# First attention of a vision tower: the next block's key and value matmuls at other chunks of the block before

## The chip, the cores and the metric

The kernel runs on one core of one Trainium2 chip. The metric is the device time of one execution in microseconds, the median of several; a profiled execution beside them gives the instructions' times. A core has TensorE (PE, with its weight loads as PEld), VectorE (DVE), ScalarE (ACT), GpSimd (POOL), each with its own in-order program, and SyncE (SP), which here issues DMAs. TensorE writes its results into PSUM, from where ACT or DVE copy them.

## What is computed

The reference is a small vision tower: a tokenizer of two convolutions gives 128 images x 64 tokens x 256 features, and two pre-norm layers follow. The change touches the attention of the first layer, which has 8 groups of 32 features and compares queries with keys by a ReLU of their difference:

```python
Q = x @ Wq.T; K = x @ Wk.T; V = x @ Wv.T            # x: (B, L, 256), normalized
diff = Q.reshape(B, L, 1, G, Dg) - K.reshape(B, 1, L, G, Dg)
attn = jnp.einsum('bqkgd,d->bqkg', jax.nn.relu(diff), w_mlp) + b_mlp[0]
attn = jax.nn.softmax(jax.nn.relu(attn), axis=2)
out = jnp.einsum('bqkg,bkdg->bqdg', attn, V.reshape(B, L, Dg, G))
```

For one image that is 64 x 64 x 256 differences, so the elementwise work and its sum over the 32 features of a group fill the stage.

## The kernel before

All of it is fp32. The activations stay in SBUF as `h2`, with two images' tokens on the 128 partitions. `relu_attention` works in eight **blocks** of 16 images, and a block in eight **chunks** of 8 query positions, 64 chunks in all. In the trace the features lie on the partitions (two halves, `hf` 0 and 1) and a tile of differences has 8 queries x some images x 64 keys.

*What a chunk does.* The `relu(q - k)` tiles of a chunk are made by three engines. DVE makes five of them in one pass each (`relu`, L570). POOL makes three differences (`difference`, L586), which ACT makes positive in six halves (`positive`, L590). ACT makes two images' parts by itself, one query at a time, in four groups of four (`by_query`, L599). PE sums every part over its features into the score tile `sc` by matmuls with a 0/weight matrix (`add`, L612, whose matmul is recorded at L417). A call of `add` sums four images. The last two adds of a chunk are `add(4, 1)` and `add(8, 1, last=True)`.

*The softmax runs one chunk later.* While chunk n is made, DVE takes the row maximum of chunk n-1's scores (`maximum`, L616, then ACT at L617), subtracts it (L621), ACT takes the exponentials (L624), DVE sums and inverts (L627, L628), POOL multiplies (L631), PE transposes the weights (L642), and one chunk later still ACT copies them to `at` (L650). PE also computes the next chunk's queries (`queries`, recorded at L424 as `pc`), which ACT copies (L510).

*What a block needs.* Before its first chunk a block needs 8 normalized row tiles (statistics L83 and L84 on DVE, factors L93 to L96 on POOL, the normalization on ACT, L109, or POOL, L107), their transposes (`transpose` L441, copied by `transposed` L447), four **key calls** (`keys`, PE, 16 records of 128x512 named `pk`, copied by ACT in `keyed`, L468), and four **value calls** (`values`, PE, 32 records of 128x256 named `pv`, copied by ACT in `valued`, L486). All keys must be there when its first chunk begins, the values when its outcome is taken. The outcome (`outcome`, L523, copied at L539) is computed in the second chunk of the block that follows, and transposed back and added to `h2` (`back` L546, `added` L556 on DVE) in that block's third and fourth chunk.

*What sets the order.* The order is written out by hand: everything runs under a manual schedule, and each engine takes its instructions in the order in which the Python calls are made. Work that is not of the chunk itself is entered with `at(n, place, ...)` for chunk n (counted over all blocks; n is the first chunk of block b in `n - 4`) and a place in the chunk's list of calls. The places that matter here, in the list's order:

- "O": on ACT after `older.transposed` (L650), ahead of the second half of `by_query(14, 1)` and of L617
- "X": on PE after the first add
- "A": on ACT after the exponentials and the fourth of the six L590
- "Y": on PE after the third add, ahead of `add(12, 1)`
- "B": on ACT after L510, ahead of the eight L599 of `by_query(15, 1)`; the add of that image stands ahead of `add(4, 1)` on PE
- "Z": on PE after the transposes of the old weights (L642), ahead of `add(8, 1, last=True)`

So the last two calls of PE in a chunk, with "Z" between them, are:

```python
ch.add(4, 1)
if old:
    old.transpose()
do(n, "Z")
...
ch.add(8, 1, last=True)
```

PSUM tiles of all this side work share four buffers (tag "pq"), used in turn. The second block's work in the first block, and the start of the layer's second part (`beside`) in the last blocks, have entries of their own.

Of the kernel before, what the change touches and what calls it, by code (L numbers as in the profile page):

```python
# [22 lines left out]
B = 128  # L23
# [357 lines left out]
def relu_attention(c, sh, ready, wqkv, wmlp, bmlp, beside):  # L381
# [10 lines left out]
    with (  # L392
# [263 lines left out]
        def at(n, place, *steps):  # L656
            work.setdefault((n, place), []).extend(steps)

        def of(f, *a):
            return lambda: f(*a)  # L660
# [18 lines left out]
        for b, x in enumerate(blocks):  # L679
            n = 8 * b  # L680

            if b + 1 < len(blocks):
                at(n + 9, "X", of(x.outcome, 0))
                at(n + 9, "A", of(x.outcome_copied, 0, 0))
                at(n + 9, "B", of(x.outcome_copied, 0, 1))
                at(n + 9, "Y", of(x.outcome, 1))
                at(n + 9, "C", of(x.outcome_copied, 1, 0))
                at(n + 10, "O", of(x.outcome_copied, 1, 1))
                for i in range(4):
                    at(n + 10 + i // 2, "XY"[i % 2], of(x.back, i))  # L690
                    at(n + 10 + i // 2, ("V1", "V2")[i % 2], of(x.added, i))
            if b == 0:
                for i in range(4):
                    at(i // 2 * 2, "XY"[i % 2], of(x.values, i))
                    at(i // 2 * 2, "AB"[i % 2], of(x.valued, i))
                continue

            if b == 1:
                at(0, "V1", *(of(x.statistics, i) for i in range(NP)))
                at(0, "W", x.factors)  # L700
                at(0, "C", of(x.normal, 0), of(x.normal, 1))
                at(1, "X", of(x.transpose, 0))
                at(1, "A", of(x.normal, 2), of(x.transposed, 0))
                at(1, "B", of(x.normal, 3))
                at(1, "Z", of(x.transpose, 1))
                at(2, "O", of(x.transposed, 1))
                for i in range(2):
                    at(n - 6 + i, "A", of(x.normal, 4 + 2 * i))
                    at(n - 6 + i, "B", of(x.normal, 5 + 2 * i))
                    at(n - 6 + i, "Z", of(x.transpose, 2 + i))  # L710
                    at(n - 5 + i, "O", of(x.transposed, 2 + i))
                for fo in range(2):
                    at(n - 4 + fo, "X", of(x.keys, 0, fo))
                    at(n - 4 + fo, "A", of(x.keyed, 0, fo))
                    at(n - 4 + fo, "Z", of(x.keys, 1, fo))
                    at(n - 3 + fo, "O", of(x.keyed, 1, fo))
                for i, (k, place) in enumerate(((5, "Y"), (4, "Y"), (2, "X"), (1, "X"))):
                    at(n - k, place, of(x.values, i))
                    at(n - k, "BA"[place == "X"], of(x.valued, i))
                continue  # L720
            for i in range(NP):
                at(n - 21 + i if b > 2 else 1 + i // 4, "V2", of(x.statistics, i))
            at(n - 13, "W", x.factors)
            for i in range(4):
                at(n - 12 + i, "A", of(x.normal, i))
                at(n - 12 + i, "C", of(x.normal, 4 + i, nc.gpsimd))
            at(n - 9, "X", of(x.transpose, 0))
            at(n - 9, "A", of(x.transposed, 0))
            at(n - 9, "Z", of(x.transpose, 2))
            at(n - 8, "O", of(x.transposed, 2))  # L730
            at(n - 8, "X", of(x.transpose, 1))
            at(n - 8, "A", of(x.transposed, 1))
            at(n - 8, "Z", of(x.transpose, 3))
            at(n - 7, "O", of(x.transposed, 3))
            at(n - 7, "Z", of(x.keys, 0, 0))
            at(n - 6, "O", of(x.keyed, 0, 0))
            at(n - 6, "Y", of(x.values, 0))
            at(n - 6, "B", of(x.valued, 0))
            at(n - 6, "Z", of(x.keys, 1, 0))
            at(n - 5, "O", of(x.keyed, 1, 0))  # L740
            at(n - 5, "Y", of(x.values, 1))
            at(n - 5, "B", of(x.valued, 1))
            at(n - 5, "Z", of(x.keys, 0, 1))
            at(n - 4, "O", of(x.keyed, 0, 1))
            at(n - 4, "X", of(x.keys, 1, 1))
            at(n - 4, "A", of(x.keyed, 1, 1))
            for i in range(2):
                at(n - 3 + i, "X", of(x.values, 2 + i))
                at(n - 3 + i, "A", of(x.valued, 2 + i))

        for (n, place), steps in beside.items():
            at(n, place, *steps)
# [1630 lines left out]
@with_exitstack  # L2383
def vit_tower(ctx: ExitStack, tc: tile.TileContext, a, out):
    const = ctx.enter_context(tc.tile_pool(name="const", bufs=1))
    dram = ctx.enter_context(tc.tile_pool(name="dram", bufs=1, space=DRAM))
    c = Ctx(tc, const)

    hd = dram.tile([B, T, D], F32, name="hd")

    hx = dram.tile([B, T, D], F32, name="hx")
    gfd = dram.tile([B * T, 1], F32, name="gfd")
    with tc.tile_pool(name="stream", bufs=1) as sp:
        c.h2 = sp.tile([P, B // 2, D], F32, name="h2")
        front = Front(c, hd, *(a[k] for k in ("wqk1", "bqk1", "wv1", "bv1", "wg")))
        with ExitStack() as rings:
            np_ = rings.enter_context(tc.tile_pool(name="an", bufs=2))
            ready = tokenizer(c, a["x"], a["w1"], a["bn1"], a["w2"], a["bn2"], np_)
            sh = Shared(c, rings, ExitStack(), np_)
            beside, rest = expert_attention(  # L2400
                c, sh, front, hd, *(a[k] for k in ("normw", "wr", "br", "wqkvf", "wvf", "wproj", "bproj", "wout"))
            )
            rest(*relu_attention(c, sh, ready, a["wqkv0"], a["wmlp"], a["bmlp"], beside))
    c.tables(ctx.enter_context(tc.tile_pool(name="tables", bufs=1)))
    with tc.tile_pool(name="gate", bufs=1) as gp:
        k = Routing(c, gp, a["wg"], a["bg"])
        with front.ctx:
            linear_attention(c, front, hd, hx, out, k)
        experts(c, hx, gfd, out, a["we1"], a["we2"], a["be2"], lambda: route(c, k, gfd))
# [70 lines left out]
```

## Time and profile before

| | us |
|---|---|
| median of 3 runs | 2536.23 |
| the three runs | 2533.86, 2536.23, 2541.09 |
| profiled execution | 2531.03 |
| its span, first to last instruction | 2529.3 |
| first attention in it, from the first L570 to the last L616 | 173 to 1040 |

The profiled execution was 5.2 us below the median. Over its span PE is busy 95%, DVE 79%, POOL 66% and ACT 65%. Those shares are means over stages: the tokenizer up to 173 us, the first attention, then the rest of the two layers. In the first attention, 173.08 to 1040.50 us, PE is busy 827 of 867 us, DVE 822, ACT 799, POOL 791. A PE instruction is recorded from its start to a modelled end, and neighbours overlap (an L417 record lasts 0.60 us and four start in every 0.43), so a busy PE is not a PE at its peak. DMA moves 3 GB/s there.

### The profile page before, as it was taken

How to read it: one execution, taken by the hardware profiler on the slowest of the kernel's cores; microseconds unless marked ns; L12 is line 12 of the kernel's file. 1: busy time of each engine (PE TensorE's matmuls, PEld its weight loads, DVE VectorE, ACT ScalarE, POOL GpSimd, SP SyncE). 2: the span in 40 equal slices, each digit the busy share in tenths (PEclk: the TensorE clock that was granted, in tenths of full speed). 3: DMA queues.
4: the chain of work that ended last, by engine and by line, in shares of the span. 5: the costliest groups of instructions: out<-in, count | busy, mean ns of one | idle time of the engine just before them, and what ended most of it. 6: DMA issues, size and time to landing. Idle time of an engine off the chain costs nothing.

```text
span 2529.3 us, 88213 instructions
## 1 busy us (share of the span) xinstructions
PE 2397.4 (95%) x38809; PEld 1613.7 (64%) x38809; DVE 2007.6 (79%) x2935; ACT 1643.9 (65%) x3529; POOL 1679.4 (66%) x1299
## 2 busy tenths in 40 slices
PE   8989999999999999899999999999999869999997
PEld 4654444444444444577777777876666657888886
DVE  7879999999999999888889898887667794444443
ACT  3239999989999998777777777775544433232332
POOL 4339998989999998588788887853322404545453
PEclk9999999999999999999999999999999989999998
DMA  4000000000000000000000000001544434555553
GB/s 126 26 14 2 3 2 3 2 3 2 2 3 2 3 14 2 3 29 22 17 14 25 14 25 14 24 14 42 103 106 109 101 108 170 194 188 196 192 195 125
DMA packets 138071, 141.57 MB, mean 56 GB/s; under 512 B 108129, under 2 KB 121859, under 8 KB 129870
## 3 DMA queue, kind: packets, MB, share of 16 engines
q1 hardware_dynamic: 128684, 119.45, 15.8%
q0 software_dynamic: 7648, 14.77, 1.9%
q8 instruction: 307, 5.03, 0.8%
q10 hardware_dynamic: 1344, 1.61, 0.2%
q14 instruction: 88, 0.72, 0.1%
HBM read 103.97 MB, written 32.54 MB: 54 GB/s over the span
## 4 chain that ended last, share of the span: by engine, by line
PE 52%; DVE 20%; POOL 11%; ACT 8%; issue 6%; DMA 1%; SPq 0%; POOLq 0%; DVEq 0%; ACTq 0%
DVE m L570 9%; PE sc L417 7%; PE po L2322 6%; PE ph L2306 6%; POOL e L1209 5%; PE pc L231 4%; PE pq L1622 3%; PE pz L1232 3%; PE pqk L1099 2%; ACT m L590 2%; PE pt L1217 2%; PE pv L1636 2%; PE pv L1122 2%; PE pk L424 2%; ACT m L599 2%
## 5 line engine op out<-in xcount | busy, mean ns | idle before, releaser
L586 POOL TENSOR_TENSOR m<-q,k 128x2048 f32<-128x2048 f32 x192 | 691.4, 3627 | 19.0 <-ACT q L510 10.1
L570 DVE CUSTOM_DVE_ANT_1 m<-pc,k 128x2048 f32<-128x2048 f32 (+1 forms) x320 | 652.9, 2059 | 0.9 <-ACT q L510 0.5
L417 PE MATMUL sc<-m,wide 128*32 128x512 f32 x4096 | 589.3, 598 | 36.1 <-ACT m L590 12.9
L590 ACT ACTIVATE m<-m 128x1024 f32<-128x1024 f32 x384 | 383.9, 1049 | 0.3
L417 PEld LDWEIGHTS sc<-m,wide 128*32 128x32 f32 x4096 | 158.2, 109 | 310.0 <-issue 178.0
L599 ACT ACTIVATE m<-k,q 128x64 f32<-128x64 f32 x1024 | 265.0, 343 | 3.9 <-DVE k L466 3.9
L1209 POOL TENSOR_TENSOR e<-e,mx 128x1024 f32<-128x1024 f32 x127 | 241.6, 1903 | 9.9
L1222 ACT COPY pT<-pt 128x512 f32<-128x512 f32 x256 | 133.4, 597 | 109.6 <-PE pt L1217 109.6
L2306 PE MATMUL ph<-xt,w1s 128*128 128x256 f32 x896 | 200.5, 382 | 1.7 <-DVE xt L2297 1.1
L2322 PE MATMUL po<-w2s,hT 128*128 128x256 f32 x896 | 198.0, 379 | 0.0
L2306 PEld LDWEIGHTS ph<-xt,w1s 128*128 128x128 f32 x896 | 171.0, 191 | 26.8 <-DVE xt L2297 1.7
L2322 PEld LDWEIGHTS po<-w2s,hT 128*128 128x128 f32 x896 | 168.1, 190 | 21.7
L2340 POOL DMA_INDIRECT out<-y,rout x56 | 56.6, 1011 | 168.1 <-ACT hT L2310 129.1
L1191 DVE TENSOR_REDUCE mx<-sc 128x16 f32<-128x1024 f32 x128 | 150.3, 1215 | 21.3 <-PE sc L1181 21.2
L1201 DVE TENSOR_REDUCE mx<-e 128x16 f32<-128x1024 f32 x128 | 154.7, 1209 | 6.3 <-ACT e L1198 4.6
L2310 ACT ACTIVATE hT<-ph,w1s 128x256 f32<-128x256 f32 x224 | 93.0, 470 | 98.6 <-PE ph L2306 98.6
L1198 ACT ACTIVATE e<-e 128x1024 f32<-128x1024 f32 x128 | 133.6, 1060 | 34.9 <-DVE e L1195 29.3
L2327 ACT ACTIVATE y<-y,gf 128x256 f32<-128x256 f32 x56 | 28.0, 507 | 194.4 <-issue 107.2
L1195 DVE TENSOR_TENSOR e<-sc,mx 128x1024 f32<-128x1024 f32 x128 | 150.1, 1213 | 0.1
L1106 ACT COPY kr<-pqk 128x512 f32<-128x512 f32 x248 | 127.3, 601 | 23.9 <-PE pqk L1099 23.8
L1217 PE MATMUL pt<-ident,e 128*128 128x128 f32 x1024 | 130.4, 277 | 12.0 <-POOL e L1209 10.8
L1232 PEld LDWEIGHTS pz<-pT,vr 128*64 128x64 f32 x4096 | 124.7, 138 | 21.1 <-issue 10.9
(347 smaller groups left out, 4796.2 us busy)
## 6 DMA issues: line engine op xcount, KB each, us to landing
w1s<-in_we SPq DMA_DIRECT2D x30, 1028.0 KB, 5.1
w2s<-in_we SPq DMA_DIRECT2D x30, 1024.0 KB, 4.9
h<-hd SPq DMA_DIRECT2D x4, 2048.0 KB, 12.2
hx<-h SPq DMA_DIRECT2D x4, 2048.0 KB, 12.2
out<-h SPq DMA_DIRECT2D x4, 2048.0 KB, 20.4
xt<-in_x SPq DMA_DIRECT2D x15, 512.0 KB, 3.7
hd<-h SPq DMA_DIRECT2D x15, 512.0 KB, 3.7
x<-hd SPq DMA_DIRECT2D x12, 512.0 KB, 3.6
```

Source lines behind the costliest of these rows:

```text
L417: nc.tensor.matmul(dst[j : j + 32], wide[:, hf, s : s + 32], part, start=start, stop=stop)
L570: nc.vector._custom_dve(TENSOR_ADD_SAT, out=m, in0=bcast(self.pc[:, o : o + n * 8].rearrange("p (t i) -> p t i", i=n), 3, T), in1=bcast(se ...
L586: nc.gpsimd.tensor_tensor(m, bcast(self.q[:, hf, s : s + 4], 3, T), k, ALU.add)
L590: nc.scalar.activation(m, m, AF.Relu)
L599: nc.scalar.activation(self.parts[i, hf][:, q], self.blk.k[:, hf, i], AF.Relu, bias=self.q[:, hf, i - NB // 2, q : q + 1],)
L1191: nc.vector.tensor_reduce(mx, self.sc[x].rearrange("p h c s -> p (h c) s"), AX.X, ALU.max)
L1201: nc.vector.tensor_reduce(self.sm[x], self.e[x], AX.X, ALU.add)
L1209: eng.tensor_mul(e, e, bcast(sm, 2, T))
L1217: nc.tensor.transpose(pt[:, cq, :], e[:, i : i + 2, :].rearrange("p e s -> p (e s)"), c.ident)
L1232: nc.tensor.matmul(pz[par * 64 : par * 64 + 64, fc, t], self.v[:, par, r % 2, 2 * fc + j, r // 2 * 64 : r // 2 * 64 + 64], self.pT[r // 2] ...
L2306: nc.tensor.matmul(ph[:, j], self.w1[:, w0 : w0 + P], self.xt[:, fc], start=(fc == 0), stop=(fc == 1))
L2322: nc.tensor.matmul(po, self.hT[:, f, r * P : r * P + P], self.w2[:, f, :], start=(f == 0), stop=(f == 7))
```

## The change

In the general schedule (blocks 3 to 8), a block's four key calls and four value calls move within the block before. With that block's chunks counted from 1:

| call | before: chunk, place (copy) | after: chunk, place (copy) |
|---|---|---|
| keys (0,0) | 2, Z (3, O) | 5, X (5, A) |
| keys (1,0) | 3, Z (4, O) | 5, Z (6, O) |
| keys (0,1) | 4, Z (5, O) | 6, Z (7, O) |
| keys (1,1) | 5, X (5, A) | 7, Z (8, O) |
| values 0 | 3, Y (3, B) | 6, X (6, A) |
| values 1 | 4, Y (4, B) | 7, X (7, A) |
| values 2 | 6, X (6, A) | 8, Y (8, B) |
| values 3 | 7, X (7, A) | own 1, Y (1, B) |

For block 2 only the value calls move: from chunk 4 (Y, B), 5 (Y, B), 7 (X, A) and 8 (X, A) of the first block to 4 (Y, B), 7 (X, A), 8 (Y, B) and its own 1 (Y, B). Nothing is added or removed.

```diff
-                for i, (k, place) in enumerate(((5, "Y"), (4, "Y"), (2, "X"), (1, "X"))):
+                for i, (k, place) in enumerate(((5, "Y"), (2, "X"), (1, "Y"), (0, "Y"))):
                     at(n - k, place, of(x.values, i))
                     at(n - k, "BA"[place == "X"], of(x.valued, i))
                 continue
...
             at(n - 7, "O", of(x.transposed, 3))
-            at(n - 7, "Z", of(x.keys, 0, 0))
-            at(n - 6, "O", of(x.keyed, 0, 0))
-            at(n - 6, "Y", of(x.values, 0))
-            at(n - 6, "B", of(x.valued, 0))
-            at(n - 6, "Z", of(x.keys, 1, 0))
-            at(n - 5, "O", of(x.keyed, 1, 0))
-            at(n - 5, "Y", of(x.values, 1))
-            at(n - 5, "B", of(x.valued, 1))
-            at(n - 5, "Z", of(x.keys, 0, 1))
-            at(n - 4, "O", of(x.keyed, 0, 1))
-            at(n - 4, "X", of(x.keys, 1, 1))
-            at(n - 4, "A", of(x.keyed, 1, 1))
+            at(n - 4, "X", of(x.keys, 0, 0))
+            at(n - 4, "A", of(x.keyed, 0, 0))
+            at(n - 4, "Z", of(x.keys, 1, 0))
+            at(n - 3, "O", of(x.keyed, 1, 0))
+            at(n - 3, "X", of(x.values, 0))
+            at(n - 3, "A", of(x.valued, 0))
+            at(n - 3, "Z", of(x.keys, 0, 1))
+            at(n - 2, "O", of(x.keyed, 0, 1))
+            at(n - 2, "X", of(x.values, 1))
+            at(n - 2, "A", of(x.valued, 1))
+            at(n - 2, "Z", of(x.keys, 1, 1))
+            at(n - 1, "O", of(x.keyed, 1, 1))
             for i in range(2):
-                at(n - 3 + i, "X", of(x.values, 2 + i))
-                at(n - 3 + i, "A", of(x.valued, 2 + i))
+                at(n - 1 + i, "Y", of(x.values, 2 + i))
+                at(n - 1 + i, "B", of(x.valued, 2 + i))
```

## The prediction

> **What bounds it now.** I read the page's 40 slices first: the first attention is the stretch from 173 to 1040 us, slices 3 to 17, where PE and DVE (and ACT and POOL) stand at 8 or 9 tenths:
>
> ```profile
> PE   8989999999999999899999999999999869999997
> DVE  7879999999999999888889898887667794444443
> ```
>
> Busy shares separate nothing there, so I cut the stretch at an event that comes once a chunk: DVE's row maximum of the chunk before, line 616. A "step into chunk n" runs from that maximum in chunk n-1 to the one in chunk n. The windows view over the eight steps of block 5 (columns: window, length, then busy us and instructions of PE, PEld, DVE, ACT, POOL, then clock, DMA share, GB/s):
>
> ```profile
> 600.60:613.69 13.09, 11.99 (x185) 5.16 (x184) 12.54 (x13) 12.78 (x31) 12.90 (x6) 1.00 0.01 1
> 613.69:626.31 12.62, 11.92 (x188) 5.10 (x184) 12.55 (x12) 12.31 (x30) 11.85 (x5) 1.00 0.01 3
> 626.31:640.36 14.05, 13.88 (x454) 8.48 (x448) 12.55 (x12) 13.45 (x32) 13.02 (x5) 1.00 0.02 4
> 640.36:654.99 14.63, 14.58 (x239) 6.89 (x232) 13.71 (x13) 12.40 (x30) 11.84 (x4) 1.00 0.01 2
> 654.99:669.62 14.63, 14.58 (x239) 6.92 (x235) 13.71 (x13) 12.40 (x30) 11.66 (x8) 1.00 0.01 3
> 669.62:682.16 12.54, 12.27 (x200) 5.98 (x196) 12.47 (x11) 12.39 (x31) 12.54 (x6) 1.00 0.01 3
> 682.16:694.70 12.54, 12.27 (x213) 6.14 (x209) 12.47 (x13) 12.23 (x30) 12.54 (x6) 1.00 0.01 1
> 694.70:707.23 12.53, 12.24 (x213) 5.96 (x205) 12.46 (x12) 12.21 (x30) 12.53 (x6) 1.00 0.01 3
> ```
>
> The steps into chunks 6 to 8 (last three) are DVE's: 12.47 of 12.54 us busy. Those into 3, 4 and 5 are longer than DVE's work by 1.50, 0.92 and 0.92. Blocks 2 to 4 have the same lengths within 0.05, but for block 2's step into 1 (13.58) and gaps in PE's issue in the steps into 3 (14.33, 15.62, 16.09). The clock is 1.00 throughout. The chain of waits, followed over the end of the step into 5, says what makes a step long (start, us, what):
>
> ```profile
> 662.17 1.92 ACT m L599 x8
> 664.14 1.11 PE sc L417 x9
> 665.45 0.59 PE sc L417
> 666.05 0.73 PE pt L642 x49
> 666.94 1.72 PE pk L424 x13
> 668.66 0.87 PE sc L417 x8
> 669.62 0.69 DVE mx L616
> ```
>
> It is a loop. The maximum lets ACT's L617 go; ACT runs in order to its eight L599, whose result PE adds (L612, shown as 417); PE then transposes the old weights (642), does whatever stands at place "Z", here a key call of 1.72, and only then the last add of the scores that the next maximum reads. Without keys the loop is just closed: at 682.16 maximum; 682.88 L617; L599 ends at 690.69; maximum at 694.70. That is 0.72 + 7.81 + 4.01 = 12.54, as long as DVE's own work. So **a key call at "Z" has nothing to hide behind in a 12.5 us step**. The first block shows this directly: in it block 2's key calls already stand at "Z" of chunks 5 and 6. Its steps into chunks 7 and 8, by the windows view, and ACT's timeline at the end of the first:
>
> ```profile
> 249.78:263.83 14.05, 13.79 (x215) 6.80 (x211) 12.55 (x11) 12.77 (x31) 12.41 (x6) 1.00 0.01 2
> 263.83:276.38 12.55, 12.29 (x216) 6.25 (x212) 12.48 (x12) 12.40 (x31) 10.83 (x6) 1.00 0.01 2
> ```
>
> ```profile
> 255.12 0.57 ACT L468 ACTIVATE k<-pk 128x512 f32<-128x512 f32 x1
> 255.59 0.59 ACT L109 ACTIVATE xn<-h,nb,rs 128x256 f32<-128x256 f32 x1
> ...
> 262.90 0.60 ACT L468 ACTIVATE k<-pk 128x512 f32<-128x512 f32 x1 [1.13 <-PE pk L424]
> ```
>
> With keys 14.05, without 12.55, DVE equally busy in both: 1.50 per key call. A PSUM copy costs ACT 0.47 (255.12 to 255.59).
>
> **The change, step by step**, for a middle block. The same instructions run; DVE, POOL and SP keep their order, no DMA moves, and each of the four shared PSUM buffers is copied out before its turn comes again, so no new wait from there.
>
> - Into chunk 3: the key call at "Z" of chunk 2 goes. Next late is DVE, 12.55: from 14.05, **-1.50**. Bounds: 0 (the 256 records of the outcome matmuls in chunk 2 keep PE the bound, as 13.88 busy hints) and -1.50. I take -1.50: in block 6 PE reaches the transposes at 743.26, and L599 lets it go no earlier (741.35 and 1.8 of adds). The gaps in PE's issue I leave as they are.
> - Into 4 and 5: a key call at "Z" and a value call at "Y" go from each, with ACT's wait of 0.95 for the value matmuls in front of L599 (662.07). Next late is DVE, whose 13.71 holds the two additions of L556: 13.75, **-0.88** twice. Bounds 0 and -0.92.
> - Into 6, 7 and 8: each gets a key call at "Z" (of chunks 5, 6, 7), and ACT the key copy at "O", behind which stand half of the L599 and L617. **+1.52** each, to 14.06. Bounds: 0 (a gain is excluded, since DVE's 12.47 stays) and +1.72, the whole call. I take the row 14.05, which has the same ACT work: two copies at "A" and the key copy.
> - Into 6 besides: GpSimd. After the normalization factors of chunk 4 POOL is busy without a break from 661.24; its second L586 of chunk 5 ends at 672.15, that is 17.16 after chunk 4's maximum. ACT wants it at 672.45, 2.83 after chunk 5's maximum. With that step 13.75 long it comes 3.41 after it: ACT waits **+0.58**. Bounds 0 and 0.58; the nearest row is the first block, where the third L590 of chunk 5 starts 1.13 after the second and not 0.95: 0.18 for POOL. I take 0.58, because the sum leaves no slack.
> - Into 1 and 2: the value copies of chunks 8 and 1 stand at "B", ahead of L599, so they lengthen ACT's part: **+0.48** each. Their matmuls are done 5.9 us after the maximum (in chunk 4 the copy starts at 661.59, 6.6 after it, with an L546 of 0.7 ahead that these don't have); ACT arrives 6.5 (chunk 8) and 6.0 (chunk 1) after it, where L599 starts today; so no wait. Bounds 0 and 0.48 + 0.95.
> - The key calls at "X" of chunk 5 and value calls at "X" of chunks 6 and 7 stand where value calls stand today in the 12.54 steps: 0, hidden in PE's wait for L599, and the 14.05 row has a key call at "X" too; 1.72 if that cover were gone.
>
> Sum: 0.48 + 0.48 - 1.50 - 0.88 - 0.88 + (1.52 + 0.58) + 1.52 + 1.52 = +2.84, three times (blocks 3 to 5) 8.5. Block 2 lacks the change into chunk 1: +2.4. Block 6 has more statistics on DVE (steps of 13.06, and 14.21 busy in the one into 5), so keys cost 1.0 and less is won into 5: +1.2. Block 7 has no statistics or normalization: keys cost 1.5 to 1.6 (11.97 to 13.58), the relieved steps end at DVE's 13.22 and POOL's 13.0: +1.4. Block 8 pays two value copies against steps of 11.96: +0.3. The first block loses a value copy and part of POOL's wait in the step into 6: -0.6. Total **+13**. The profiled execution took 2531.0 (span 2529.3), so 2544; the median of the runs shown is 2536.2, 5.2 above it, so **2549**.
>
> [...] The row says a key call costs 1.50 of its 1.72. [...]
>
> **Rivals.**
> - *PE's load is what counts, and it is evened out* (faster). Steps into 3 to 5 have PE busy to the end, those into 6 to 8 leave it waiting 0.27 and more for L599; keys fill that room and only the gains stay: -3.26 in blocks 2 to 5, -2.8 and -3.8 in 6 and 7, -0.6: about -20, **2516**. It decides if the steps into 6 to 8 stay under 12.7. Against it: 14.05 in the first block.
> - *Only the keys count*: ACT hides the "B" copies and the POOL wait does not come. Each middle block is 1.54 cheaper, +1.3; in all +6, **2542**. For it: in the step into 2 ACT is busy 12.31 of 12.62.
> - *The waits are worse*: value copies wait 0.95 at "B" as they do today in chunk 3, and keys cost 1.72: 2 x 0.95 + 3 x 0.2 = 2.5 a block more, +13, **2562**. For it: the "Y" place is the same. Against: there ACT has no other copy to do first.
> - *Nothing moves*: the built order shows the calls at their new places; only a hidden common bound would keep 2536.
>
> **Chances.** Forecast 0.60, first rival 0.12, second 0.17, third 0.09, nothing 0.02. A measurement can tell about 0.3%, 7.6 us, from no change. The first rival is faster, 0.11; the second, the last and the lower edge of the forecast are within, 0.21; the rest is slower, 0.68. The range leaves out the first rival and the far end of the third: 2537 to 2561.
>
> **What would show it.** In the profile after: steps into 6 to 8 at about 14, with ACT's L468 waiting 1.1 for pk; steps into 3 near 12.6, into 4 and 5 near 13.75 with DVE's wait at L616 gone; 13.5 into 1. I am wrong if L616 in chunks 6 to 8 has no wait for PE, or if steps 4 and 5 stay at 14.6 because PE is late for another reason.

## The result and the profile after

The kernel after took 2551.59 us, the median of 5 runs (2546.21 to 2552.82), against 2536.41 (2533.86 to 2541.09) for the kernel before: ratio 1.0051, 95% interval 1.0035 to 1.0067, which is +9 to +17 us. The forecast was 2549, slower by 13. The profiled execution of after took 2552.82 (span 2551.1) and was the longest of its runs, while before's was shorter than any of those five; so the two profiles are 21.8 apart and the medians 15.2.

The first attention, from the first L570 to the last L616, went from 867.38 to 880.76 us: **+13.4**. A second profile of each kernel, told of below, gave 866.93 and 880.78. By blocks the difference is -0.6, +2.6, +4.2, +2.0, +2.9, +1.3, +0.4, +0.7.

The two lines of the page's slices that were shown of before, now of after, look the same, because PE and DVE were nearly full and still are:

```profile
PE   8999999999999999899999999999999869999997
DVE  7879999999999999888889888887667794444443
```

The windows view does show the change. The eight steps of block 5 (columns as before: window, length, busy us and instructions of PE, PEld, DVE, ACT, POOL, then clock, DMA share, GB/s):

```profile
609.13:622.72 13.59, 12.89 (x220) 5.98 (x216) 12.56 (x12) 13.45 (x33) 11.87 (x6) 1.00 0.01 1
622.72:635.82 13.10, 12.86 (x220) 5.98 (x216) 12.55 (x12) 12.79 (x31) 11.85 (x5) 1.00 0.01 3
635.82:648.36 12.54, 12.54 (x440) 7.51 (x432) 12.47 (x11) 12.26 (x29) 11.24 (x5) 1.00 0.02 5
648.36:662.05 13.69, 13.35 (x193) 5.99 (x188) 13.62 (x15) 12.39 (x32) 12.36 (x5) 1.00 0.01 3
662.05:675.74 13.69, 13.10 (x192) 5.36 (x196) 13.62 (x15) 11.24 (x27) 11.45 (x9) 1.00 0.00 1
675.74:690.49 14.75, 12.47 (x199) 5.58 (x195) 12.63 (x12) 12.28 (x28) 14.75 (x6) 1.00 0.01 2
690.49:704.56 14.07, 13.80 (x231) 7.04 (x227) 12.56 (x11) 12.80 (x31) 13.02 (x6) 1.00 0.01 2
704.56:718.62 14.06, 13.79 (x231) 7.01 (x224) 12.55 (x11) 12.79 (x31) 12.36 (x6) 1.00 0.01 2
```

Read the lengths beside DVE's column. In the third to fifth line DVE is busy to within 0.07 of the step: they fell to DVE's work, from 14.05, 14.63 and 14.63. In the last three DVE has 1.5 us and more to spare: the loop through ACT and PE is longer again. The chain of waits over the step into chunk 7 shows that loop with the key call in it:

```profile
697.11 1.93 ACT m L599 x8
...
699.08 1.11 PE sc L417 x9
...
701.88 1.72 PE pk L424 x13
703.60 0.87 PE sc L417 x8
...
704.56 0.70 DVE mx L616
```

This is the chain that stood in the steps into 4 and 5 before, with the same 1.72. It only comes later in the block. Before, the step into 7 (682.16 to 694.70) had no key call at "Z", and its chain ended on DVE alone:

```profile
690.29 4.17 DVE m L570 x2
694.46 0.24 issue
694.70 0.68 DVE mx L616
```

In after, ACT's timeline has the copy of the key call (start, length, line, and in brackets the idle time ahead of it and what ended it):

```profile
703.63 0.60 ACT L468 ACTIVATE k<-pk 128x512 f32<-128x512 f32 x1 [1.13 <-PE pk L424]
```

### The profile page after: what moved, and what is told of

Same layout as the page of the kernel before. It is cut to its first block, busy times and chain, and to the rows that moved or that the text cites. A ratio compares the mean times of both kernels' runs of the same rounds, so it can differ in the third digit from the quotient of the medians.

```text
span 2551.1 us, 88251 instructions
## 1 busy us (share of the span) xinstructions
PE 2408.9 (94%) x38809; PEld 1616.6 (63%) x38809; DVE 2009.0 (79%) x2935; ACT 1642.6 (64%) x3529; POOL 1680.8 (66%) x1299
## 4 chain that ended last, share of the span: by engine, by line
PE 51%; DVE 18%; ACT 12%; POOL 11%; issue 7%; DMA 1%; SPq 0%; POOLq 0%; DVEq 0%; ACTq 0%
DVE m L570 7%; PE sc L417 6%; PE po L2322 6%; PE ph L2306 6%; POOL e L1209 4%; PE pc L231 4%; ACT m L590 4%; PE pq L1622 3%; PE pz L1232 3%; PE pqk L1099 2%; PE pt L1217 2%; ACT m L599 2%; PE pv L1122 2%; PE pv L1636 2%; PE pt L642 2%
## 5 line engine op out<-in xcount | busy, mean ns | idle before, releaser
L586 POOL TENSOR_TENSOR m<-q,k 128x2048 f32<-128x2048 f32 x192 | 691.3, 3630 | 16.0 <-ACT q L510 10.3
L570 DVE CUSTOM_DVE_ANT_1 m<-pc,k 128x2048 f32<-128x2048 f32 (+1 forms) x320 | 652.9, 2059 | 1.5 <-PE sc L417 1.0
L417 PE MATMUL sc<-m,wide 128*32 128x512 f32 x4096 | 598.7, 600 | 40.9 <-ACT m L590 16.7
L590 ACT ACTIVATE m<-m 128x1024 f32<-128x1024 f32 x384 | 384.7, 1051 | 2.5 <-POOL m L586 2.3
L599 ACT ACTIVATE m<-k,q 128x64 f32<-128x64 f32 x1024 | 265.6, 346 | 3.9 <-DVE k L466 3.9
L1191 DVE TENSOR_REDUCE mx<-sc 128x16 f32<-128x1024 f32 x128 | 150.3, 1215 | 21.1 <-PE sc L1181 20.6
```

The costliest lines, as they stand in the source:

```text
L417: nc.tensor.matmul(dst[j : j + 32], wide[:, hf, s : s + 32], part, start=start, stop=stop)
L570: nc.vector._custom_dve(TENSOR_ADD_SAT, out=m, in0=bcast(self.pc[:, o : o + n * 8].rearrange("p (t i) -> p t i", i=n), 3, T), in1=bcast(se ...
L586: nc.gpsimd.tensor_tensor(m, bcast(self.q[:, hf, s : s + 4], 3, T), k, ALU.add)
L590: nc.scalar.activation(m, m, AF.Relu)
L599: nc.scalar.activation(self.parts[i, hf][:, q], self.blk.k[:, hf, i], AF.Relu, bias=self.q[:, hf, i - NB // 2, q : q + 1],)
L1191: nc.vector.tensor_reduce(mx, self.sc[x].rearrange("p h c s -> p (h c) s"), AX.X, ALU.max)
```

## The experiments

All of them change only the entries of `at` in the schedule of the side work, but for the two with extra transposes. Each ratio is to runs of the kernel before on the same chip (their medians are 2535.4 to 2536.5). "Behind" is the stage from the last L616 to the last L1191, the attention of the second layer, which no experiment edits.

| kernel | median, us (runs) | ratio and 95% interval | first attention | behind |
|---|---|---|---|---|
| before | 2536.41 (5) | | 867.4 | 690.7 |
| after | 2551.59 (5) | 1.0051, 1.0035 to 1.0067 | 880.8 | 695.3 |
| keys alone | 2551.51 (6) | 1.0058, 1.0037 to 1.0079 | 875.2 | 700.3 |
| keys alone, again | 2554.59 (4) | 1.0066, 1.0041 to 1.0091 | 875.3 | 700.7 |
| values alone | 2535.93 (10) | 0.9998, 0.9985 to 1.0011 | 864.6 | 696.5 |
| after, keys at "Y" | 2527.48 (10) | 0.9956, 0.9944 to 0.9969 | 855.6 | 696.3 |
| after, factors early | 2547.16 (7) | 1.0038, 1.0021 to 1.0056 | 876.8 | 697.0 |
| after, copies late | 2548.77 (9) | 1.0047, 1.0030 to 1.0063 | 875.4 | 697.7 |
| spread | 2520.42 (6) | 0.9937, 0.9916 to 0.9958 | 846.9 | 700.8 |
| spread, rows too | 2517.14 (6) | 0.9923, 0.9905 to 0.9942 | 843.9 | 703.1 |
| extra transposes, first block | 2539.69 (10) | 1.0016, 0.9999 to 1.0032 | 868.4 | 699.5 |
| extra transposes, last block | 2539.62 (10) | 1.0017, 1.0002 to 1.0031 | 867.7 | 696.7 |
| before, again | 2536.14 (1) | | 866.9 | 691.7 |
| after, again | 2558.22 (1) | | 880.8 | 698.7 |

### Each half of the change alone

The theory is the prediction's: a key call at "Z" costs about 1.5 wherever it stands in a step that DVE bounds, and value copies at "B" cost 0.5. The rival is its first rival: PE's load is evened out and the later steps have room.

**Keys alone**: the keys at their new places, the values at their old ones.

```diff
-                for i, (k, place) in enumerate(((5, "Y"), (2, "X"), (1, "Y"), (0, "Y"))):
+                for i, (k, place) in enumerate(((5, "Y"), (4, "Y"), (2, "X"), (1, "X"))):
...
-            at(n - 3, "X", of(x.values, 0))
-            at(n - 3, "A", of(x.valued, 0))
...
-            at(n - 2, "X", of(x.values, 1))
-            at(n - 2, "A", of(x.valued, 1))
...
-            for i in range(2):
-                at(n - 1 + i, "Y", of(x.values, 2 + i))
-                at(n - 1 + i, "B", of(x.valued, 2 + i))
+            at(n - 6, "Y", of(x.values, 0))
+            at(n - 6, "B", of(x.valued, 0))
+            at(n - 5, "Y", of(x.values, 1))
+            at(n - 5, "B", of(x.valued, 1))
+            at(n - 3, "X", of(x.values, 2))
+            at(n - 3, "A", of(x.valued, 2))
+            at(n - 2, "X", of(x.values, 3))
+            at(n - 2, "A", of(x.valued, 3))
```

> Only the key calls move (to chunks 5 to 7, as in the changed kernel); the value calls stay where they were before. Theory (a key call at Z delays the next maximum by 1.5 us, and a relieved step ends at DVE's work): in blocks 3 to 5 steps of 13.1, 12.6, 12.5, 13.7, 13.7, 14.75, 14.06, 14.06, which is 108.5 against 106.6 before; in all about +7 us on before. The value copies at B in chunks 3 and 4 cost nothing now, since DVE's 13.7 covers them. Rival (PE's load decides): PE is relieved in chunks 2 to 4 and has room in 5 to 7, so faster than before by about 12 us.

Measured: 875.2 us in the first attention, +7.8; block 5 in steps of 13.11, 12.62, 12.55, 13.69, 13.69, 14.76, 14.07, 14.06, in all 108.55. The theory holds there, and the rival, which wanted a gain, falls. The median rose by twice as much as the attention, which the theory does not give, so the kernel was run a second time.

> The same kernel as e1_keys_alone a second time, since its first attention grew by the 8 us of the theory but its median by 15. If the other 7 us came from the stages after it by chance, the median comes out near 2544; if they belong to the kernel, at 2551 again.

It gave the same attention, 875.27, and again more outside it: 700.7 in the stage behind. What that is comes up in the last group of experiments.

**Values alone**: the values at their new places, the keys back at their old ones, block 2 as after.

```diff
-            at(n - 4, "X", of(x.keys, 0, 0))
-            at(n - 4, "A", of(x.keyed, 0, 0))
-            at(n - 4, "Z", of(x.keys, 1, 0))
-            at(n - 3, "O", of(x.keyed, 1, 0))
+            at(n - 7, "Z", of(x.keys, 0, 0))
+            at(n - 6, "O", of(x.keyed, 0, 0))
+            at(n - 6, "Z", of(x.keys, 1, 0))
+            at(n - 5, "O", of(x.keyed, 1, 0))
+            at(n - 5, "Z", of(x.keys, 0, 1))
+            at(n - 4, "O", of(x.keyed, 0, 1))
+            at(n - 4, "X", of(x.keys, 1, 1))
+            at(n - 4, "A", of(x.keyed, 1, 1))
...
-            at(n - 3, "Z", of(x.keys, 0, 1))
-            at(n - 2, "O", of(x.keyed, 0, 1))
...
-            at(n - 2, "Z", of(x.keys, 1, 1))
-            at(n - 1, "O", of(x.keyed, 1, 1))
```

> Only the value calls move; the key calls stay at Z of chunks 2 to 4. Theory: steps into 1 and 2 longer by 0.48 each (13.57, 13.10), into 4 and 5 down to DVE's 13.7 although the key calls are still there (a key at Z without other copies on ACT makes a loop of 13.1, under 13.7), into 6 about 13.2 because POOL's factors are then late, into 7 and 8 as before: about 106.4 a block against 106.6, in all within 2 us of before. So either half of the move wins the 0.9 of steps 4 and 5 by itself, and the whole change wins it once only. If costs simply add up, keys alone minus 6 and values alone plus 6 would have to give the measured +13 differently: values alone +5.

Measured: 864.6, or -2.8; block 5 at 13.58, 13.11, 14.06, 13.70, 13.69, 13.17, 12.54, 12.54, in all 106.38. Two things follow. The value copies do cost 0.5 in each of the steps into 1 and 2 (13.58 for 13.09, 13.11 for 12.62), so the second rival, in which ACT hides them, falls. And the steps into 4 and 5 reach DVE's 13.69 in *both* halves: taking away either the key call or the value call suffices. If the halves added, they would make +7.8 - 2.8 = +5.0, and not +13.4. Block 5 shows why they don't: +1.92 and -0.25 make +1.67, against +2.87 in after. The gain in the steps into 4 and 5, 1.87, is in both halves and can be had only once; the wait in the step into 6 (13.17 for 12.54, 0.63) is also in both. 1.67 + 1.87 - 0.63 = 2.91.

### Is it PE's load, or the place in the loop?

The kernel after, with the three "Z" calls at "Y", ahead of the wait for L599, in the same chunks. PE's work per chunk is the same.

```diff
-            at(n - 4, "Z", of(x.keys, 1, 0))
+            at(n - 4, "Y", of(x.keys, 1, 0))
-            at(n - 3, "Z", of(x.keys, 0, 1))
+            at(n - 3, "Y", of(x.keys, 0, 1))
-            at(n - 2, "Z", of(x.keys, 1, 1))
+            at(n - 2, "Y", of(x.keys, 1, 1))
```

> The changed kernel with its three key calls moved from Z to Y in the same chunks (5, 6, 7), their copies unchanged at O of the next chunk: the same work of PE and ACT in the same chunks, only in front of the wait for L599 instead of between the transposes and the last add. Theory (place in the loop): steps into 7 and 8 fall from 14.06 to 12.6 to 12.8, into 6 from 14.75 to about 13.2 (POOL's 0.59 stays); about 25 us less than the changed kernel, 2526, and faster than before. Rival (PE's load in these chunks is the price): 14.06 stays, no change.

Measured: 855.6 in the first attention, 25 us less than after, and a median below that of before. Block 5's step into 6 fell from 14.75 to 13.16. The windows view of this kernel over block 5's steps into chunks 7 and 8:

```profile
674.09:686.71 12.62, 12.62 (x230) 7.60 (x224) 12.55 (x12) 12.59 (x32) 12.62 (x6) 1.00 0.01 3
686.71:699.33 12.62, 12.62 (x231) 7.46 (x221) 12.55 (x12) 12.59 (x32) 12.62 (x6) 1.00 0.01 2
```

PE carries 230 and 231 matmul records, as after does (231) in its 14.07, in 1.45 us less. So there was room on PE for the keys, as the first rival said; the calls were only put where that room can't be used. At "Z" a call comes behind the wait for L599 and ahead of the last add; at "Y" it fills the wait. It fills it to the end: the chain of waits runs on PE alone, without a wait, from one key call to the next 12.63 us later, while DVE is 0.07 short of the step:

```profile
679.04 1.72 PE pk L424 x16
...
691.67 1.72 PE pk L424 x16
```

So a call of 1.72 costs 0.08 at "Y" in these steps (12.62 for before's 12.54), against 1.53 at "Z". By this chain PE is at its limit there. No run here puts more than these calls into such a step.

### GpSimd's factors

The kernel after, with the normalization factors (L93 to L96) entered one place earlier on POOL, so that they run ahead of the softmax's L631 and not behind it.

```diff
-            at(n - 13, "W", x.factors)
+            at(n - 13, "A", x.factors)
```

> The changed kernel with the normalization factors on POOL moved within chunk 4 from behind the softmax weights (W) to in front of them (A), where POOL waits 1.9 us for DVE. Theory (POOL's lateness costs 0.59 in the step into 6): ACT's wait of 0.59 before the third L590 of chunk 5 goes, the step falls from 14.75 to 14.06 to 14.16 in blocks 2 to 5; about 3 to 4 us less in all. If POOL was not the cause the step stays at 14.75.

Measured: 876.8, or 4.0 less than after; every step into chunk 6 of blocks 2 to 5 is 14.05 to 14.07, where after has 15.19, 15.47, 14.76, 14.75. Of the 4.0, some 1.2 are what after's steps of 15.19 and 15.47 have over its 14.76 and 14.75: two stretches at a granted clock of 0.50 (told of below). POOL's timeline around chunk 4 of block 5, in after and then in this kernel:

```profile
668.28 1.04 POOL L631 TENSOR_TENSOR e<-e,mx 128x512 f32<-128x512 f32 x1 [1.90 <-DVE mx L628]
669.42 0.24 POOL L93 TENSOR_SCALAR rs<-mv 128x8 f32<-128x8 f32 x1
...
672.00 10.79 POOL L586 TENSOR_TENSOR m<-q,k 128x2048 f32<-128x2048 f32 x3
```

```profile
664.40 0.24 POOL L93 TENSOR_SCALAR rs<-mv 128x8 f32<-128x8 f32 x1
...
666.98 1.04 POOL L631 TENSOR_TENSOR e<-e,mx 128x512 f32<-128x512 f32 x1
667.98 10.79 POOL L586 TENSOR_TENSOR m<-q,k 128x2048 f32<-128x2048 f32 x3
```

In after POOL idles 1.90 for DVE's L628 and then does the factors. Early, they fill the idle time. ACT in chunk 5 of after shows what that delay costs, and PE behind it:

```profile
679.24 1.06 ACT L590 ACTIVATE m<-m 128x1024 f32<-128x1024 f32 x1 [0.59 <-POOL m L586]
```

```profile
682.01 2.73 PE L417 MATMUL sc<-m,wide 128*32 128x512 f32 x18 [2.01 <-ACT m L590]
```

### The copies at "B"

The kernel after, with the copies of value calls 2 and 3 behind the eight L599 instead of ahead of them.

```diff
-                at(n - 1 + i, "B", of(x.valued, 2 + i))
+                at(n - 1 + i, "C", of(x.valued, 2 + i))
```

> The changed kernel with the copies of values 2 and 3 moved from B (ahead of the eight L599) to C (behind them), in the same chunks 8 and 1. Theory (a copy at B costs 0.48 because it delays L599, which PE waits for): the step into 1 falls from 13.59 to 13.2 or 13.3, into 2 from 13.10 to 12.8, as a copy behind L599 only uses up ACT's wait of 0.28 before L617; some 3 us less in all than the changed kernel. Rival (ACT is simply full, wherever the copy stands): 13.59 and 13.10 stay.

Measured: 875.4, or 5.4 less than after. Block 5's steps into 1 and 2 are:

```profile
607.56:620.67 13.11, 12.89 (x220) 5.92 (x216) 12.56 (x11) 13.00 (x32) 11.38 (x6) 1.00 0.01 1
620.67:633.29 12.62, 12.62 (x220) 6.08 (x216) 12.55 (x11) 12.58 (x31) 11.86 (x5) 1.00 0.01 3
```

That is before's 13.09 and 12.62 with the value calls and their copies still in them: behind L599 a copy costs nothing, and the 0.1 to 0.2 left for it in the expectation was too much. The price at "B" is the place, not ACT's load. The medians of this kernel and of factors early lie 3 and 4 us below after's, with intervals that overlap after's, so both verdicts rest on the steps; stretches at a clock of 0.50 and gaps in PE's issue, which differ from one profile of after to the other (told of below), may have a part in the 5.4.

### A version that beats both

If the place decides, the eight calls should be spread over the places that lie in PE's wait for L599 ("X" and "Y"), and their copies kept off "B". "Spread" does that: the entries below stand in the place of after's keys and values, block 2's are as before, and the factors are early; "rows too" also moves the two row transposes that stand at "Z".

```diff
-            at(n - 13, "W", x.factors)
+            at(n - 13, "A", x.factors)
...
+            at(n - 6, "X", of(x.keys, 0, 0))
+            at(n - 6, "A", of(x.keyed, 0, 0))
+            at(n - 5, "X", of(x.keys, 1, 0))
+            at(n - 5, "A", of(x.keyed, 1, 0))
+            at(n - 4, "X", of(x.keys, 0, 1))
+            at(n - 4, "A", of(x.keyed, 0, 1))
+            at(n - 3, "X", of(x.keys, 1, 1))
+            at(n - 3, "A", of(x.keyed, 1, 1))
+            at(n - 4, "Y", of(x.values, 0))
+            at(n - 3, "O", of(x.valued, 0))
+            at(n - 3, "Y", of(x.values, 1))
+            at(n - 2, "O", of(x.valued, 1))
+            at(n - 2, "X", of(x.values, 2))
+            at(n - 2, "A", of(x.valued, 2))
+            at(n - 2, "Y", of(x.values, 3))
+            at(n - 1, "O", of(x.valued, 3))
```

> Neither order: keys at X of chunks 3 to 6 with copies at A, values at Y of 5, 6, 7 (copies at O of the next) and at X of 7, block 2 as before, factors early. Nothing of a block stands at Z but two row transposes, nothing at B. Theory: steps of 13.1, 12.6, 12.55, 13.7, 13.7, 12.6, 12.6, 12.6, 103.5 a block against 106.6 before; about 20 us less than before, 2516. Rival (PE's load): the chunks 3 and 4 have PE filled up again, so steps 4 and 5 go back to 14.6 and the whole is no faster than before.

Measured: 846.9; block 5 at 13.23, 12.62, 12.55, 13.69, 13.69, 12.53, 12.56, 12.61, in all 103.48 against 106.63 before and 109.50 after. The 20 us of the expectation came in the attention (-20.5), but the median fell by only 15.0, to 2520.42 and not 2516. What is left over DVE's work in the step into 1 are the row transposes at "Z":

```diff
-            at(n - 9, "Z", of(x.transpose, 2))
+            at(n - 9, "Y", of(x.transpose, 2))
...
-            at(n - 8, "Z", of(x.transpose, 3))
+            at(n - 8, "Y", of(x.transpose, 3))
```

> e6_spread with the two row transposes moved from Z to Y as well (chunks 8 and 1), copies unchanged at O. Theory (anything at Z, also 0.6 us of transposes, adds to the loop): the step into 1 falls from 13.1 to 12.6, into 2 from 12.62 to 12.55; 3 us less than e6_spread, about 2513. Rival: 13.1 has another cause (two copies on ACT in chunk 8) and stays.

Measured: 843.9, 3.0 less than spread, and a median of 2517.14, the lowest of all: 0.9923 of before (0.9905 to 0.9942, which overlaps spread's interval; the expectation had about 2513). The steps into 1 and 2 are 12.62 both, so the rival, two copies on ACT, falls. Its steps into chunk 1 and 7 by the windows view:

```profile
589.28:601.90 12.62, 12.36 (x190) 5.24 (x184) 12.55 (x12) 12.58 (x32) 12.34 (x6) 1.00 0.00 1
666.96:679.52 12.56, 12.56 (x228) 7.58 (x224) 12.49 (x12) 12.53 (x31) 12.35 (x6) 1.00 0.01 3
```

Every step of block 5 is now within 0.08 us of DVE's busy time, and in the second line PE and ACT are as full as DVE, and POOL nearly.

### What lies outside the first attention

Keys alone had 7 to 11 us more in its medians than its attention explains. Every other edited kernel also had more, by 1 to 6 us: spread, rows too, won 23.5 in its attention and 18.3 in the medians. Nothing outside is edited by the change. Do small shifts ahead of it move the stage behind? Two kernels repeat 16 transposes of rows, early or late, in the kernel before; then both kernels were profiled once more as they are.

```diff
                     for n in range(2):
-                        nc.tensor.transpose(
-                            pt[:, fc, n], self.xn[:, 2 * i + n, fc * P : fc * P + P], c.ident
-                        )
+                        for _ in range(2 if self.b0 == 0 else 1):
+                            nc.tensor.transpose(
+                                pt[:, fc, n], self.xn[:, 2 * i + n, fc * P : fc * P + P], c.ident
+                            )
```

The second kernel has `self.b0 == 112`, the last block.

> The kernel before with the 16 transposes of the first block's rows (L441) issued twice, which changes nothing that is computed and nothing in the order after it. It asks how much the time outside the first attention moves when nothing there is edited: the keys-alone kernel had 700.3 and 700.7 us from the last L616 to the last L1191, the kernel before 690.7, with the same instructions in the same order. Theory (the length of that stage changes with small shifts of everything ahead of it, so that differences of some us between any two kernels lie outside the edit): the stage is 3 us or more away from 690.7, and the median with it, while the first attention stays at 867 within 3. Rival (the stage feels only what the keys' places leave behind): 690.7 within 1, and the median 2536 to 2539, only the some 2 us of the added transposes.

> The kernel before with the 16 transposes of the last block's rows (L441) issued twice, in chunks 1 and 2 of block 7, with nothing else edited. As for the extra transposes of the first block, but with the shift put in late: theory (small shifts ahead of it change the later stage): 3 us or more away from 690.7 from the last L616 to the last L1191; rival: 690.7 within 1, the median 2536 to 2538. The first attention 867 to 869 by both.

> The kernel before, unchanged, profiled once more: what one kernel's stages differ by from execution to execution. Theory (the stage behind the first attention varies by itself, and the first profile of before happened to catch it short): more than 693 us from the last L616 to the last L1191, with the first attention again at 867 within 2. Rival (a kernel's own later stage is fixed, and only edited kernels shift it): 690.7 within 1.

> The kernel after, unchanged, profiled once more. By both theories the first attention is 880.8 within 3 (its steps into chunks 6 of blocks 2 to 5 at 14.75, two of them perhaps with a half-clock stretch); by the theory that the later stage varies by itself that stage is off 695.3 by some us, by the rival within 1.

Measured: with the transposes the stage behind was 699.5 and 696.7, 6 to 9 above before's 690.7, as the theory said; but the medians rose by only 3.3, so as to the time of many runs it fails. The two profiled executions were 7.7 and 3.6 above the medians of their kernels, so part of those 6 to 9 may belong to the execution. Before, profiled again, gave 691.7, which is the rival's answer within its 1 us; after gave 698.7 in place of 695.3, which is the theory's. The question stays **open**: the stage differs by 12 us between kernels that share it, partly from one execution to the next, and part of it comes back with a kernel (keys alone, twice). One profile of it can't be set against another to better than some 3.4 us, which is what after's two differ by. The first attention came back within 0.5 us in each of the three kernels that were profiled twice, so the verdicts above rest on it.

## Why the prediction was right

The total of the sum, +13, met +13.4 in the stage and +15 in the medians (+9 to +17). The terms of a middle block were right one by one, as block 5 shows (+2.87 for +2.84). That the total came within half a microsecond is luck as well: blocks 3 and 8 were 1.4 and 0.4 over their terms, blocks 4 and 7 were 0.9 and 1.0 under theirs. Two stretches at a clock of 0.50, in blocks 2 and 3, are in the measured total with 1.2 and not in the sum. Its parts:

- **Into chunk 3**: -1.50 predicted, 14.05 to 12.54 = -1.51 measured in block 5, the end of the range that had DVE next. The gaps in PE's issue, which were left as they are, did not stay: block 3 went from 15.61 to 14.70 where the rule for block 5 gives 14.1, block 4 from 16.10 to 13.66. They moved from profile to profile of the same kernel too (16.10 and 16.29 before, 13.66 and 14.07 after, in block 4).
- **Into 4 and 5**: -0.88 each predicted, -0.94 measured; DVE's 13.62 ends them, as was said. Either half of the change would have brought it.
- **Into 6 to 8, the keys**: +1.52 predicted, 12.54 to 14.07 = +1.53. The whole call, 1.72, was the upper bound, and the chain after has all 1.72 in it. The step pays less because the loop without a call is 14.07 - 1.72 = 12.35, not the 12.54 that the prediction read off: in the steps without keys the chain runs on DVE alone, as the lines from before's step into 7 show (above, under the result). PE's timelines agree: its next call after the transposes starts 11.02 after the maximum in before (the last add, 682.16 to 693.18) and 11.03 in after (the key call, 690.49 to 701.52), but from the start of the last add to the next maximum it takes 1.52 in before (693.18 to 694.70) and 1.32 in after (703.24 to 704.56). So before's maximum came about 0.19 later than the loop would have let it go. So the working "0.72 + 7.81 + 4.01, as long as DVE's own work" had a wait for DVE in its last term, and the row of the first block gave the right price all the same.
- **Into 6, POOL**: +0.58 predicted; ACT waited 0.59, and the step was 0.68 over its neighbours. The second L586 ended 17.17 after chunk 4's maximum (662.05 to 679.22), predicted 17.16. Its reading "busy without a break from 661.24" holds. What it left out lies just ahead of that: POOL waits for L628 there, 2.56 in before and 1.90 in after, and that is why moving the factors ahead of the wait was free. What it missed is the clock: 0.89 over the steps of 15.19 and 15.47, below.
- **Into 1 and 2**: +0.48 each predicted, +0.50 and +0.48 measured, no wait at "B".
- **Blocks**: block 5 is +2.87 for +2.84, block 6 +1.30 for +1.2, block 2 +2.6 for +2.4, the first block -0.6 for -0.6. Block 8 has +0.7 for +0.3: its value copies cost 0.33, and its step into 3 another 0.4. Block 3 has +4.2 and block 4 +2.0 instead of +2.84: gaps in PE's issue and, in block 3, a stretch at a clock of 0.50. Block 7 was mis-sized: +0.4 for +1.4. Its relieved steps fell to 12.35, 13.17 and 13.16 from 14.04, 14.63 and 14.63, the first of them below the 13.0 that the prediction had as POOL's, and its step into 2 got shorter by 0.16, not longer by 0.48.
- **The rivals**: the first (2516) fell by its own condition: the steps into 6 to 8 are 14.07 and more, not under 12.7. Yet its ground was sound, as the keys at "Y" show. The second and third fell with the 0.5 at "B".

## What to carry to other kernels

In a loop across in-order engines, a piece of side work is priced by its place in the loop, not by how full its engine looks: behind the last wait of a step it costs its whole length less the slack of the loop (1.53 of 1.72 here), and ahead of that wait next to nothing as long as the wait is there to be filled (0.08). Before moving work to an "emptier" step, ask which place in that step it takes; and where two calls make the same step late, see whether moving one of them already wins the whole gain, as it did here.

## What the runs showed of the hardware

**Behind PE waits of 2.0 us the granted clock was 0.50 for a while in some steps and 1.00 throughout in others.** In after, PE waits 2.00 to 2.02 for L590 in chunk 5 of blocks 2 to 5. In blocks 2 and 3 the windows view shows a lower clock behind it, here the step into chunk 6 of block 2, and then the part of it at half clock:

```profile
342.79:357.98 15.19, 13.19 (x198) 6.41 (x194) 12.64 (x13) 12.29 (x28) 15.19 (x6) 0.89 0.01 2
349.60:353.00 3.40, 3.40 (x24) 0.99 (x19) 3.37 (x4) 3.40 (x13) 3.40 (x4) 0.50 0.02 7
```

Block 3's step of 15.47 has 0.50 from 462.20 to 465.60. Blocks 4 and 5, each behind a wait of 2.01, have 1.00 throughout and steps of 14.76 and 14.75. In after profiled again block 5 has the lower clock, behind a wait of 2.00: its step is 15.56, at 0.89. In factors early the wait in block 5 is 1.31 in place of 2.01, and the step has 1.00. The start of the stage shows the same both ways: in the first chunk of block 1 PE waits 2.08 for L570 in before, with 0.50 from 187.40 to 190.70 behind it, and 2.09 in after, with 1.00 behind it. No run here shows what decides it. In chunk 5 the stretch cost 0.4 to 0.8 us of a step (15.19, 15.47 and 15.56 beside 14.75).

**The same matmuls at the same places issue with different gaps** in the second chunk of a block (the outcome matmuls): in before the steps into 3 of blocks 2 to 5 were 14.33, 15.62, 16.09 and 14.05, with 452 to 454 matmul records each, and in block 4 the chain of waits has 1.50 of "issue" at 524.90. Block 4's step into 3 was 13.66 and 14.07 in two profiles of after. No run here shows why.
